# Layer 2's quotients: from two VectorE instructions to eight ScalarE ones, in a task of their own

## The chip, the cores and the metric

The kernel runs on one core of one Trainium2 chip. The metric is the device time of one execution in microseconds (us). A core has several engines, each with its own queue of instructions that it works through in order: TensorE (PE, matrix products; PEld is its weight loading), VectorE (DVE), ScalarE (ACT, which evaluates func(scale x + bias)), GpSimd (POOL) and SyncE (SP, which issues DMAs). Engines wait for one another through semaphores. PE writes its products into PSUM, from which DVE and ACT read.

## The reference

Four graph layers run one after another over x of shape (16, 1024, 64) with one 1024x1024 adjacency. Each is `x = layernorm(x + layer(x))`. Layers 0 and 2 are graph attention with an additive score:

```
h = x @ W;  s1 = h @ a1;  s2 = h @ a2
e = leaky_relu(s1[:, :, None] + s2[:, None, :], 0.2)
attention = softmax(where(adj > 0, e, NEG), axis=-1)
x = layernorm(x + elu(attention @ h))
```

Layer 1 averages softplus features with a softmax of their own over the neighbours, and layer 3 is a four-head attention with scores h h^T followed by an output attention. The change lies in layer 2.

## The kernel before

**Layers.** `fast_path` computes layers 0 to 3 in sequence; a general path behind a flag is not taken with these inputs. In the profile layer 2 lies between 461 and 688 us, and layer 3 takes the rest.

**Layer 2's work.** `gat_layer` is used for layers 0 and 2; layer 2 has `zero_mean=True`. Nodes lie on 128 partitions in C=8 chunks of 128. For one batch b there are eight *units*, one for each chunk k of source nodes: DVE makes `e = max(G, q) * aT` of 128x1024 (L965), where G and q hold the exponentials that factor exp(leaky_relu(s1+s2)) and aT is the transposed adjacency. PE then multiplies `vals` (x weighted by p) with e into a PSUM accumulator y (L977). After eight units the batch has its unnormalised result, and a list of *ends* finishes it:

- `evict`: ACT copies y from PSUM to SBUF (L996)
- `project`: PE multiplies by the weight, eight products of 128x130 into a PSUM tile `po`, columns 128 and 129 being the sums of the softmax (L1009)
- `divide`: DVE clamps the sums (L1034) and takes reciprocals rt (L1036), two DVE multiplications make the quotients v = po*rt (L1039), and ACT makes m = exp(v) (L1046)
- `residual`: two DVE operations, elu and x added (L1051, L1052)
- `norm`: DVE's bn_stats for eight chunks (L1060); for an odd b also the moments of both batches of a pair
- `root`, `shift`: for an odd b, ACT's Ln and Exp for the inverse root (L703, L704), and DVE's refinement and shift
- `store`: ACT writes the normalised x, eight activations of 128x64 (L776)

**Preparation.** For each pair of batches: `prep_x` (PE transposes, ACT copies, L904, L905), `prep_s` (PE, L911), `prep_top` (DVE maximum, then a reduction over partitions on POOL, L922), `prep_p` (DVE L928, L930, ACT exponentials p and q, L933, L935), `prep_G` in two halves (PE product pg, L945, and ACT exponential into G, L946; pg has one buffer), and `prep_v` (ACT, eight activations with a pointer scale, L952, and a copy, L954). The first e of an even batch needs both halves of G.

**Order.** The order on every engine is the order of the program, written out by hand in slots (t, k): t is the round, 0 to 16, and k the unit, 0 to 7. In slot (t, k) DVE makes unit k of batch t, PE multiplies the unit made two units before (LAG = 2), and then the tasks of the slot are issued: ends first, by batch, then preparation, then extras. An end of batch b at place (1, 4) is issued in slot (b+1, 4). Ends with places after the parameter `own` in round 16 (5 before) are handed on and issued in the first bursts of layer 3. Layer 3's first preparation is in slots (15, 0) to (15, 7), and the last rows of layer 1 in (0, 0) to (1, 7).

The places of the preparation for a pair starting at b, relative to b, are:

```
places = (-2, 0), (-2, 1), (-2, 5), (-2, 6), (-2, 7), (-1, 1), (-1, 4), (-1, 6), (-1, 2), (0, 4)
```

in the order prep_x 0 and 1, prep_s lower and upper, prep_top, prep_p, prep_G 0 and 1, prep_v of b and of b+1.

Of the kernel before, what the change touches and what calls it, by code (L numbers as in the profile page):

```python
# [12 lines left out]
AF = mybir.ActivationFunctionType  # L13
# [565 lines left out]
def fast_path(  # L579
# [24 lines left out]
    nc = tc.nc  # L604
# [8 lines left out]
    CH = C // 2  # L613
# [136 lines left out]
    def moments(st):  # L750


        n = st.shape[1]
        t = {k: small.tile([P, n], F32, tag=f"bn_{k}", name=f"bn_{k}") for k in ("mean", "d", "var", "rstd", "shift")}
        v = nc.vector
        v.tensor_tensor(t["d"], st[:, :, 1], st[:, :, 4], ALU.subtract)
        v.tensor_tensor(t["var"], st[:, :, 2], st[:, :, 5], ALU.add)
        v.tensor_tensor(t["mean"], st[:, :, 1], st[:, :, 4], ALU.add)

        v.scalar_tensor_tensor(t["d"], t["d"], 0.25, t["d"], ALU.mult, ALU.mult)  # L760
        v.tensor_scalar(t["var"], t["var"], 1.0 / D, LN_EPS, ALU.mult, ALU.add)
        v.tensor_tensor(t["var"], t["var"], t["d"], ALU.add)
        root, step = inverse_root(t["rstd"], t["var"])

        def finish():
            step()
            v.scalar_tensor_tensor(t["shift"], t["mean"], -0.5, t["rstd"], ALU.mult, ALU.mult)  # L767
            return t["rstd"], t["shift"]

        return root, finish  # L770
# [114 lines left out]
    def gat_layer(w, name, zero_mean, extra, first, own, ordered):  # L885
# [74 lines left out]
        def attention(b):  # L960
            held = {}
# [69 lines left out]
            def divide():  # L1031
                pos, tot = held["p"]
                total = sums[:, b, :]
                nc.vector.tensor_scalar(total.rearrange("p (h t c) -> p t c h", h=2, t=2), tot, 1e-30, None, ALU.max)  # L1034
                rt = small.tile([P, C], F32, tag="rt", name="rt")
                nc.vector.reciprocal(rt, total)  # L1036
                held["v"] = ep.tile([P, C, D], F32, tag="v", name="v")
                for h, po in enumerate(pos):
                    nc.vector.tensor_tensor(  # L1039
                        held["v"][:, h * CH : (h + 1) * CH, :].rearrange("p (t c) d -> p t c d", t=2), po,  # L1040
                        rt[:, h * CH : (h + 1) * CH].rearrange("p (t c) -> p t c", t=2).unsqueeze(3).to_broadcast(
                            [P, 2, 2, D]
                        ), ALU.mult,
                    )
                held["m"] = ep.tile([P, C, D], F32, tag="m", name="m", bufs=4)
                nc.scalar.activation(held["m"], held["v"], AF.Exp)  # L1046
# [25 lines left out]
            def store():  # L1072
                rows = slice(b % 2 * C, (b % 2 + 1) * C)
                scaled(xb(b), held["m"], [t[:, rows] for t in stats[b // 2]["n"]], range(C))

            return unit, product, [evict, project, divide, residual, norm, root, shift, store]

# [3 lines left out]
        def at(t, k, task):  # L1083
            slots.setdefault((t, k), []).append(task)

        work = [attention(b) for b in range(B)]
        if zero_mean:
            ends = [(1, 1), (1, 3), (1, 4), (1, 6), (1, 7), (2, 0), (2, 2)]
            ends = [*ends, (3, 6)], [*ends, (3, 2)]
        else:  # L1090

            ends = (
                [(1, 3), (1, 5), (1, 7), (2, 0), (2, 1), (2, 1), (2, 1), (4, 0)],
                [(1, 3), (1, 7), (2, 1), (2, 2), (2, 3), (2, 5), (2, 7), (3, 4)],
            )
# [28 lines left out]
        for t in range(B + 1):  # L1124
            for k in range(C):
                catch_up()
                if t < B:
                    unit, product, _ = work[t]
# [348 lines left out]
    with tc.tile_pool(name="ps_g", bufs=1, space=bass.MemoryType.PSUM, reuse_waits="tile") as ps_g, tc.tile_pool(  # L1477
        name="ps_u", bufs=2, space=bass.MemoryType.PSUM, reuse_waits="tile"
    ) as ps_u, tc.tile_pool(name="gat0", bufs=2, reuse_waits="tile") as gp:
        later = {}  # L1480

        def first(ahead):
            with tc.tile_pool(name="stage", bufs=2, reuse_waits="tile") as stage:
                tiles = load_adj(stage)
                load_x(2)
                load_x(3)
                later["w2"] = gat_weights(L2_W, L2_a, "l2", True, nc.sync)
                later["w3"] = layer3_weights(gp)
                for b in range(4, B):
                    load_x(b)  # L1490
                for c in range(C):
                    adjacency(stage, tiles[c], c)
                    for task in ahead[c : c + 1]:
                        task()
                for task in ahead[C:]:
                    task()

        extra = {(0, 6): [lambda: gat_setup(later["w2"], "l2", True)], (1, 2): [lambda: later["w3"]()]}
        ending = gat_layer(w_0, "l0", False, extra, first, 5, True)
# [14 lines left out]
    with tc.tile_pool(name="l1", bufs=2, reuse_waits="tile") as l1, tc.tile_pool(  # L1514
# [55 lines left out]
        def product_l1(g, ic):  # L1570
            po = ps_a.tile([P, 2, 2, P], F32, tag="acc", name=f"po{g}_{ic}")
            for k in range(C):
                for e in (his[g], los[g]):
                    nc.tensor.matmul(  # L1574
                        po.rearrange("p q k f -> p (q k f)"), aR[:, k, ic * P : (ic + 1) * P],
                        e[:, k].rearrange("p q k f -> p (q k f)"),
                        start=(k == 0 and e is his[g]), stop=(k == C - 1 and e is los[g]),
                    )
            return po
# [15 lines left out]
        for g in range(NG):  # L1595
            ahead = prep_l1(g + 1) if g + 1 < NG else [[] for _ in range(C)]
            st = l1.tile([P, C * GB, 6], F32, tag="st1", name=f"st{g}")
            for ic in range(C):
                po = product_l1(g, ic)
# [6 lines left out]
            root, finish = moments(st)  # L1606
# [30 lines left out]
    for b in range(B):  # L1637
# [6 lines left out]
        ends = outs[b][1][1]  # L1644
# [37 lines left out]
    with tc.tile_pool(name="ps_g", bufs=1, space=bass.MemoryType.PSUM, reuse_waits="tile") as ps_g, tc.tile_pool(  # L1682
        name="ps_p", bufs=1, space=bass.MemoryType.PSUM, reuse_waits="tile"
    ) as ps_p, tc.tile_pool(
        name="gat2", bufs=2, reuse_waits="tile"
    ) as gp:
        places = [(15, j) for j in (0, 1, 2, 3, 4, 5, 6, 7)]
        extra = {p: [task] for p, task in zip(places, ahead)}
        for p, task in zip(((0, 0), (0, 1), (0, 3), (0, 7), (1, 3), (1, 7)), last):
            extra.setdefault(p, []).append(task)  # L1690

        def first(ahead):
            for task in ahead:
                task()

        ending = gat_layer(later["w2"], "l2", True, extra, first, 5, True)
    for j, task in enumerate(ending):
        at(0, j, task)

# [81 lines left out]
def kernel(tc, *args):  # L1781


    nc = tc.nc
    with tc.tile_pool(name="flag", bufs=1) as fp:
        redo = fp.tile([1, 1], I32, tag="redo", name="redo")
        fast_path(tc, redo, *args)
        again = nc.values_load(redo[0:1, 0:1], min_val=0, max_val=1)
        with tc.If(again == 1):
            general_path(tc, *args)  # L1790
# [32 lines left out]
```

## Time and profile before

| | |
|---|---|
| median of three runs | 2103.89 us (2102.4 to 2103.98) |
| profiled execution, its own time | 2103.7 us |
| its span, first to last instruction | 2101.4 us |
| busy over the span: PE, DVE, ACT | 94%, 88%, 59% |
| layer 2's e (L965 covers layers 0 and 2) | 256 times, 1277 ns each |
| quotients, L1039 (layers 0 and 2: L1039 is 64 instructions) | 24.2 us |

A row of a group names the line, engine and operation, output <- inputs with shapes, the count, then busy us and the mean ns of one, then the time its engine sat idle just before it and what ended that. The mean of one instruction is longer than the distance between two in a row, because an engine starts the next before the last is through. A row of the timeline has start and length in us, then the same names; neighbouring instructions of a kind are merged (x5). An idle time and its releaser stand in brackets.

### The profile page before, as it was taken

How to read it: one execution, taken by the hardware profiler on the slowest of the kernel's cores; microseconds unless marked ns; L12 is line 12 of the kernel's file. 1: busy time of each engine (PE TensorE's matmuls, PEld its weight loads, DVE VectorE, ACT ScalarE, POOL GpSimd, SP SyncE). 2: the span in 40 equal slices, each digit the busy share in tenths (PEclk: the TensorE clock that was granted, in tenths of full speed). 3: DMA queues.
4: the chain of work that ended last, by engine and by line, in shares of the span. 5: the costliest groups of instructions: out<-in, count | busy, mean ns of one | idle time of the engine just before them, and what ended most of it. 6: DMA issues, size and time to landing. Idle time of an engine off the chain costs nothing.

```text
span 2101.4 us, 26433 instructions
## 1 busy us (share of the span) xinstructions
PE 1969.2 (94%) x10065; PEld 858.0 (41%) x10065; DVE 1845.0 (88%) x3160; ACT 1237.7 (59%) x2029; POOL 69.7 (3%) x77
## 2 busy tenths in 40 slices
PE   6999979989888999999999999999999999999983
PEld 3444347863332343343434334333434343433431
DVE  5888989989999778798898898989989889888997
ACT  4355556645555766666666656656665665665541
POOL 0000000000000000000000000000000000000001
PEclk7999989999999999999999999999999999999997
DMA  7000000000000100000000000000000000000000
GB/s 167 1 1 1 1 1 1 1 1 1 0 1 11 51 21 1 1 1 6 1 5 6 1 6 1 6 6 1 6 1 6 6 1 6 6 1 6 1 5 17
DMA packets 23656, 18.91 MB, mean 9 GB/s; under 512 B 19361, under 2 KB 19426, under 8 KB 23522
## 3 DMA queue, kind: packets, MB, share of 16 engines
q1 hardware_dynamic: 23218, 17.11, 3.0%
q8 instruction: 81, 1.33, 0.3%
q14 instruction: 53, 0.43, 0.1%
q10 hardware_dynamic: 304, 0.03, 0.0%
HBM read 12.95 MB, written 4.19 MB: 8 GB/s over the span
## 4 chain that ended last, share of the span: by engine, by line
PE 45%; DVE 41%; ACT 10%; issue 3%; DMA 0%; POOL 0%; SPq 0%; POOLq 0%; DVEq 0%; ACTq 0%
DVE e L1290 12%; PE y L1297 11%; PE s L1282 8%; DVE e L965 7%; ACT e L1286 6%; PE y_l L977 6%; DVE junk L1392 4%; DVE e L1403 4%; PE u_l L989 3%; PE po L1574 3%; PE po L1312 2%; PE y L1412 2%; ACT e L1387 2%; DVE v L1322 1%; PE s L1382 1%
## 5 line engine op out<-in xcount | busy, mean ns | idle before, releaser
L1286 ACT ACTIVATE e<-s,shift 128x1024 f32<-128x1024 f32 x512 | 542.8, 1119 | 335.0 <-PE s L1282 334.2
L1290 DVE TENSOR_TENSOR e<-e,aT 128x1024 f32<-128x1024 f32 x512 | 600.4, 1217 | 1.7 <-ACT e L1286 1.6
L1282 PE MATMUL s<-hT 64*128 64x512 f32 x2048 | 495.1, 603 | 1.2 <-ACT e L1286 0.9
L1297 PE MATMUL y<-e,vals 128*64 128x512 f32 x2048 | 488.7, 599 | 5.8 <-ACT yT L1303 4.3
L965 DVE SCALAR_TENSOR_TENSOR e<-G_l,q,aT 128x1024 f32<-128x1024 f32 x256 | 315.3, 1277 | 7.2 <-ACT G_l L946 7.2
L1282 PEld LDWEIGHTS s<-hT 64*128 64x128 f32 x2048 | 185.7, 186 | 278.0 <-issue 138.9
L977 PE MATMUL y_l<-e,vals_l 128*64 128x512 f32 x1024 | 261.2, 634 | 25.3 <-DVE e L965 24.4
L1297 PEld LDWEIGHTS y<-e,vals 128*64 128x64 f32 x2048 | 134.7, 136 | 272.4 <-issue 190.7
L1392 DVE SCALAR_TENSOR_TENSOR junk<-e,aN 128x1024 bf16<-128x1024 f32 x128 | 155.8, 1217 | 0.0
L1403 DVE TENSOR_TENSOR e<-e,aT 128x1024 f32<-128x1024 f32 x120 | 147.0, 1225 | 6.4
L1387 ACT ACTIVATE e<-s,shift 128x1024 f32<-128x1024 f32 x128 | 142.1, 1116 | 1.2 <-PE s L1382 1.1
L1382 PE MATMUL s<-h2T 64*128 64x512 f32 x512 | 131.6, 595 | 0.0
L977 PEld LDWEIGHTS y_l<-e,vals_l 128*64 128x64 f32 x1024 | 64.8, 141 | 162.5 <-issue 73.1
L1412 PE MATMUL y<-e,h2v 128*64 128x512 f32 x480 | 123.4, 592 | 2.7 <-DVE e L1403 2.7
L1574 PE MATMUL po<-hi,aR 128*128 128x512 f32 x256 | 101.9, 398 | 2.7 <-ACT hi L1559 1.1
L1574 PE MATMUL po<-lo,aR 128*128 128x512 f32 x256 | 99.8, 390 | 0.0
L776 ACT ACTIVATE x<-m,bn_shift,bn_rstd 128x64 f32<-128x64 f32 x256 | 88.3, 430 | 0.5 <-DVE bn_shift L767 0.5
L1225 POOL PARTITION_ALL_REDUCE gtop<-top x48 | 42.5, 885 | 1367.0 <-DVE top L1223 1298.8
L1312 PE MATMUL po<-wb,yT 128*128 128x130 f32 x512 | 74.2, 288 | 10.1 <-ACT e L1286 9.4
L1312 PEld LDWEIGHTS po<-wb,yT 128*128 128x128 f32 x512 | 61.9, 190 | 47.4 <-ACT e L1286 45.8
L1382 PEld LDWEIGHTS s<-h2T 64*128 64x128 f32 x512 | 49.7, 188 | 61.2 <-issue 28.8
L1316 DVE COPY sums<-po 128x8 f32<-128x8 f32 x64 | 10.9, 170 | 71.8 <-PE po L1312 71.8
(217 smaller groups left out, 2059.1 us busy)
## 6 DMA issues: line engine op xcount, KB each, us to landing
adj<-in_adj_dram SPq DMA_DIRECT2D x16, 512.0 KB, 4.2
x<-in_x_dram SPq DMA_DIRECT2D x16, 256.0 KB, 5.2
out_dram<-res SPq DMA_DIRECT2D x16, 256.0 KB, 2.0
wl<-in_L_gnn_Wh_dram SPq DMA_DIRECT2D x2, 64.0 KB, 3.6
wo<-in_L_gnn_Wo_dram SPq DMA_DIRECT2D x1, 64.0 KB, 3.1
l_wd<-in_L_gnn_W_dram ACTq DMA_DIRECT2D x2, 16.0 KB, 3.9
l_wd<-in_L_gnn_W_dram SPq DMA_DIRECT2D x2, 16.0 KB, 2.0
bo<-in_L_gnn_bo_dram SPq DMA_DIRECT2D x1, 32.0 KB, 3.1
```

The lines of the kernel that those rows point to most:

```text
L965: nc.vector.scalar_tensor_tensor(e, G[b - b % 2][:, b % 2, :], pq[b - b % 2][1][:, k, b % 2 : b % 2 + 1], aT[:, k, :], ALU.max, ALU.mult,)
L977: nc.tensor.matmul(held["y"][h * D : (h + 1) * D, :], vals[b][:, k, :], e[:, h * HALF : (h + 1) * HALF], start=(k == 0), stop=(k == C - 1),)
L1282: nc.tensor.matmul(s[:, i, :], hT[rows, k * P : (k + 1) * P], hT[rows, cols], start=True, stop=True)
L1286: nc.scalar.activation(e, s, AF.Exp, bias=shifts[b, n])
L1290: nc.vector.tensor_tensor(e, e, bc_mid(aT[:, k, h * HALF : (h + 1) * HALF], 2), ALU.mult)
L1297: nc.tensor.matmul(held[h][i * D : (i + 1) * D, :], vals[b][:, k, :], e[:, i, :], start=(k == 0), stop=(k == C - 1),)
L1312: nc.tensor.matmul(o[:, j // 2, j % 2, :], held["y"][:, j * P : (j + 1) * P], wb[:, n, :], start=True, stop=True,)
L1382: nc.tensor.matmul(s[:, i, :], hT[rows, (i + k // CH) % 2, k % CH * P : (k % CH + 1) * P], hT[rows, 0, :], start=True, stop=True,)
L1387: nc.scalar.activation(e, s, AF.Exp, bias=shifts[b])
L1392: nc.vector.scalar_tensor_tensor(junk.rearrange("p c q -> p (c q)").bitcast(BF16), e.rearrange("p i q -> p (i q)"), 1.0, aN[:, k, :], ALU. ...
L1403: nc.vector.tensor_tensor(m, e, aT[:, k, :].rearrange("p (i q) -> p i q", i=2), ALU.mult)
L1574: nc.tensor.matmul(po.rearrange("p q k f -> p (q k f)"), aR[:, k, ic * P : (ic + 1) * P], e[:, k].rearrange("p q k f -> p (q k f)"), start ...
```

## The change

In layer 2 `divide` keeps the clamp and the reciprocal. The quotients become a task `quotients` of their own: eight ACT activations (Copy with the scale taken from a column of rt) from PSUM into v, then m = exp(v) as before. In layer 0, `divide` calls `quotients` at once and nothing else differs. The places of layer 2's ends are new: evict (1,1), project (1,3) and divide (1,4) stay; quotients (1,5); residual from (1,6) to (2,0); norm from (1,7) to (2,1); for odd b root from (2,0) to (2,3), shift from (2,2) to (2,5), store from (3,2) to (3,4); for even b root and shift do nothing, and the store goes from (3,6) to (4,0). `own` goes from 5 to 6, so that the last batch's quotients still belong to layer 2. The same six tasks as before are handed on to layer 3.

```diff
                 nc.vector.reciprocal(rt, total)
                 held["v"] = ep.tile([P, C, D], F32, tag="v", name="v")
+                held["r"] = rt
+                if not zero_mean:
+                    quotients()
+
+            def quotients():
+                pos, rt = held["p"][0], held["r"]
                 for h, po in enumerate(pos):
+                    if zero_mean:
+
+                        for j in range(CH):
+                            c = h * CH + j
+                            nc.scalar.activation(
+                                held["v"][:, c, :], po[:, j // 2, j % 2, :], AF.Copy, scale=rt[:, c : c + 1]
+                            )
+                        continue
                     nc.vector.tensor_tensor(
                         held["v"][:, h * CH : (h + 1) * CH, :].rearrange("p (t c) d -> p t c d", t=2), po,
...
-            return unit, product, [evict, project, divide, residual, norm, root, shift, store]
+            ends = [evict, project, divide, residual, norm, root, shift, store]
+            if zero_mean:
+                ends.insert(3, quotients)
+            return unit, product, ends
...
         if zero_mean:
-            ends = [(1, 1), (1, 3), (1, 4), (1, 6), (1, 7), (2, 0), (2, 2)]
-            ends = [*ends, (3, 6)], [*ends, (3, 2)]
+            ends = [(1, 1), (1, 3), (1, 4), (1, 5), (2, 0), (2, 1)]
+            ends = [*ends, (2, 1), (2, 1), (4, 0)], [*ends, (2, 3), (2, 5), (3, 4)]
...
-        ending = gat_layer(later["w2"], "l2", True, extra, first, 5, True)
+        ending = gat_layer(later["w2"], "l2", True, extra, first, 6, True)
```

## The prediction

> **What bounds the kernel now.** I read the page first, then busy time by stretch, to find layer 2 (461 to 688 us), then its waits and groups, and last the timeline of one pair of batches. By stretch (columns: length; busy PE, PEld, DVE, ACT, POOL; granted PE clock; DMA):
>
> ```profile
> 484.94:654.86 169.92, 147.70 (x672) 55.51 (x668) 167.09 (x359) 92.62 (x272) 7.41 (x6) 0.94 0.00 1
> 654.86:687.73 32.87, 26.73 (x128) 9.70 (x128) 29.54 (x73) 19.80 (x55) 1.59 (x2) 0.95 0.06 17
> ```
>
> The first row is six pairs of batches (t=2 to 13), 28.32 us each: VectorE (DVE) is busy 98%, ScalarE (ACT) 55%. The second is t=14 to the first exponential of layer 3. What DVE waited for in the first row, and groups of that row:
>
> ```profile
> DVE l_sums L1034 <- PE po L1009: 0.3, 1, 0.3
> ...
> L965 DVE SCALAR_TENSOR_TENSOR e<-G_l,q,aT 128x1024 f32<-128x1024 f32 x96 | 118.6, 1277 | 0.0
> L952 ACT ACTIVATE vals_l<-x,p 128x63 f32<-128x63 f32 x96 | 24.0, 332 | 0.0
> L1039 DVE TENSOR_TENSOR v<-po,rt 128x256 f32<-128x256 f32 x24 | 9.1, 419 | 0.4
> L1046 ACT ACTIVATE m<-v 128x512 f32<-128x512 f32 x12 | 7.6, 631 | 36.4 <-DVE v L1039 36.4
> ```
>
> DVE waits once, 0.3 us in 170. So layer 2 is a DVE queue without gaps, and a DVE instruction taken out shortens it until something else arrives late. The candidate stands in the timeline, second half of a pair (t odd):
>
> ```profile
> 506.06 0.17 DVE L1034 TENSOR_SCALAR l_sums<-po 128x8 f32<-128x8 f32 x1
> 506.16 1.13 PE L945 MATMUL pg<-xT_l,l_w 64*128 64x512 f32 x4
> 506.26 0.20 DVE L1036 RECIPROCAL rt<-l_sums 128x8 f32<-128x8 f32 x1
> 506.50 0.76 DVE L1039 TENSOR_TENSOR v<-po,rt 128x256 f32<-128x256 f32 x2
> 507.17 2.47 DVE L965 SCALAR_TENSOR_TENSOR e<-G_l,q,aT 128x1024 f32<-128x1024 f32 x2
> 507.29 0.63 ACT L1046 ACTIVATE m<-v 128x512 f32<-128x512 f32 x1 [2.96 <-DVE v L1039]
> 507.83 1.10 ACT L946 ACTIVATE G_l<-pg,up 128x1024 f32<-128x1024 f32 x1
> 508.82 2.75 ACT L776 ACTIVATE x<-m,bn_shift,bn_rstd 128x64 f32<-128x64 f32 x8
> 511.48 1.09 ACT L946 ACTIVATE G_l<-pg,up 128x1024 f32<-128x1024 f32 x1
> 513.11 6.05 DVE L965 SCALAR_TENSOR_TENSOR e<-G_l,q,aT 128x1024 f32<-128x1024 f32 x5
> ```
>
> The next pair's first e (513.11) reads all of G, whose second half ends at 512.57: 0.54 us to spare. Last, the end of the layer, where ACT carries the path, and the PE clock in two stretches:
>
> ```profile
> 684.08 0.57 ACT L996 COPY yT_l<-y_l 128x512 f32<-128x512 f32 x1
> 684.55 2.76 ACT L776 ACTIVATE x<-m,bn_shift,bn_rstd 128x64 f32<-128x64 f32 x8
> ...
> 687.21 0.61 ACT L1046 ACTIVATE m<-v 128x512 f32<-128x512 f32 x1
> 687.73 5.10 ACT L1286 ACTIVATE e<-s,shift 128x1024 f32<-128x1024 f32 x5
> ```
> ```profile
> 498.94:500.94 2.00, 0.27 (x2) 0.30 (x4) 1.97 (x5) 0.82 (x3) 1.24 (x1) 0.85 0.00 0
> 500.94:502.94 2.00, 2.00 (x6) 0.48 (x5) 2.00 (x4) 1.12 (x5) 0.00 (x0) 0.50 0.00 0
> ```
>
> **The change, part by part.** Below, t is the round of the loop and times are starts, in us.
>
> *Removed from DVE.* Two quotients a batch. From l_sums to the next e it is 506.06 to 507.17, 1.11 us; without the quotients the e follows the reciprocal's start by about 0.10 (independent small operations start 0.10 apart), so 0.30. Saved: 0.81 a batch, 1.62 a pair.
>
> *Added on ACT.* Eight activations with one pointer scale. Nearest row: L952, eight of 128x63 with one pointer, 2.00 us, 0.2375 apart. Upper end: L776, two pointers, eight from 508.82 to 511.48, 0.333 apart. Lower end: ACT copies 128x512 from PSUM in 576 to 599 ns against 631 for L1046 from SBUF, so up to 0.045 less, 0.19. The operation is L952's, so I take 0.2375, 2.00 for eight. The exponential starts 0.03 later (L703 and L704, dependent, start 0.24 apart with 0.216 each) and lets the next in after 0.54. ACT's load becomes 15.4+2x1.9=19.2 of 26.6 us a pair, 72%: no bound by volume.
>
> The Trainium skill, "ScalarE: Activation LUTs", Rules for kernel authors, says to give a multiplication to VectorE, not ScalarE. Per element the rows agree (0.84 us on DVE, 2.00 on ACT), and by that rule alone the sum would be 16x(2.00-0.81)=19 us slower, an estimate that takes all of it as exposed.
>
> *Moved.* Residual, bn_stats, root, shift and store come one to two slots later. Their instructions are the same; no DMA moves, and POOL's reduction stays. What matters is what they no longer cover. At t odd DVE had, between the divide and the next pair's first e, three e's, the residual (1.33: 509.56 to 510.89) and bn_stats (1.02). Now residual and bn_stats come before e1 and e2, and the shift (0.71) comes after e5. The new t odd, e's 1.195 apart (chain: 5.97 for five): e0 at 0, residual 1.20, e1 2.53, bn_stats and moments 3.72 (2.02), down/up 5.74 (0.13), e2 5.87, e3 7.07, e4 8.26, divide 9.46, e5 9.76, shift 10.95, e6 11.66, e7 12.86, and the next e0 at **14.05**. The new t even is 12.51 (e's 9.56, residual 1.33, bn_stats 1.02, divide 0.30, top 0.30). The pair: 26.56 against 28.17, the undisturbed period (484.94 to 513.11).
>
> *The new wait.* When is G ready? PE takes product(e2) 0.05 after e2 ends (5.87+1.28), 7.20; pg follows 1.01 later (505.15 to 506.16), 8.21, lasts 1.13; first half of G on ACT at 9.39. ACT is free then: p, q and eight vals from 5.92 to 8.34, root to 8.85. Then, in ACT's order: quotients at 9.39+0.99=10.38 (the reciprocal was done at 9.86), exponential 12.41, second half of G 12.95, done 14.05, seen by DVE 14.09 (0.04 as at 461.11 to 461.15). Wanted at 14.05: a wait of **0.04** a pair. Slack has gone to nothing, and every further us is paid six times. What queues behind the quotients on ACT is that half of G; who waits is e0, and behind it all DVE.
>
> At t even nothing waits: two stores, copies and vals hold ACT until 8.9, the quotients follow the reciprocal (8.7), m is ready near 11.6, and the residual wants it at 13.7. PE, at t even, does 12.0 of work in 12.51 and its backlog drains in t odd.
>
> *Start.* At t=1 no residual yet stands before the divide (it ran at 477.90), so e0 of t=2 is wanted at 477.90+0.30+3x1.195=481.79. ACT: rows of x at 476.77 end 479.42, G's first half, quotients 480.41, exponential 482.44, second half 482.98 to 484.08, seen 484.12. The wait is 2.33; e0 comes at 484.12 instead of 484.94: -0.82, while residual and bn_stats of batch 0 (2.35) are still owed.
>
> *Six pairs.* 6x(28.17-26.56)=-9.66, and 6x0.04=+0.24 waits.
>
> *End.* Before, 32.87 from t=14's first e to layer 3's first exponential. Now t=14 is 12.21; in t=15 e7 is at about 12.9 and the second maximum at 14.1. ACT then: its shift 14.83 (POOL between), the store of batch 12 (now behind it; it ran at 680.10 in ACT's idle time) 15.03, yT 17.68, store of 13 at 18.15 to 20.80, quotients of 15 (reciprocal ready at 19.9), exponential 22.83, layer 3's first at 23.37. Sum 35.58: **+2.71**. It holds the owed 2.35 on DVE, which ACT's queue covers.
>
> Sum: -0.82-9.66+0.24+2.71=**-7.5 us**. Layer 3 starts that much earlier and runs on unchanged. The profiled execution took 2103.7 (span 2101.4, and 2.3 around it), 0.2 below the median of 2103.89: 2103.7-7.5=**2096.2**.
>
> With x the extra time of a batch's eight quotients over 2.00, the total is -7.5+8x: six pairs, start and end all pay it. Pitch 0.333 gives x=0.76, 2102.3; pitch 0.19 gives start and end 0.37 each and the waits of 0.24 back, 2095.2.
>
> **Rivals.** 0.2% is 4.2 us, about what a measurement here can tell from no change.
>
> *A, within 0.2%: G late by half a us to 1.4 in each pair.* Through x above 0.41, or through PE at half clock. The two clock rows show 0.50 after PE had sat 2.53 us before one product; that gap (bn_stats and moments with nothing else) is gone. The new gaps, 1.28 before product(e1) and 1.25 before product(e2), are shorter than 1.64 (before 650.73), after which it stayed 1.00, but the clock did fall after 1.70 (before 669.76). If it falls at product(e2), that and pg (1.7 and 1.84 in slow rows) put G 1.4 late: -7.5+6x1.4, 2104.6. The Trainium skill, "TensorE: Matmul & The Clock Gate", Part 1, throttles only after an idle window of about 3.4 us; by that it would not fall here, yet the trace has it falling after 2.53.
>
> *B, slower: the quotients do not overlap.* They write one tile out of shared banks and might run one after another as L703 and L704 do. At L952's 0.332+0.03 each, x=0.9, 2103.4, still A; at L776's 0.430+0.03, x=1.65, 2109.4. It decides from a pitch of about 0.42, x=1.46. Against it: L952's eight also write one tile, and overlap.
>
> *C, ACT is the path throughout.* The quotients' 2.00 is paid where 0.81 was saved, 19 us over sixteen batches: 2122.7. Against it: at t even m has two us to spare, and ACT's 55%. This is the ScalarE rule's outcome.
>
> **How the numbers follow.** My forecast 0.64, all of it faster; A 0.18, within (x from 0.41 to 1.46, or G late by as much); B 0.14, slower (x above 1.46); C 0.04, slower. Faster 0.64, same 0.18, slower 0.18. The forecast's own range is 2093 to 2099.5: x from -0.3 to 0.4, and an end between +1 and +3.5. For eight in ten the range reaches through A to 2106; below 2092.5 I leave 0.03.
>
> **What would show it.** Quotients 0.24 apart on ACT; a pair of about 26.6 us; e0 of each even batch waiting for G under 0.3 us, 2.3 at t=2; no 2.5 us PE gap; layer 3's first exponential near 680.2. Wrong if e0 waits over 1 us for G in every pair, if the clock is 0.50 at product(e2), or if DVE waits for a residual's m.

## The result

The changed kernel takes 2096.86 us (median of six, 2093.37 to 2097.86) against 2103.14 for the kernel before: ratio 0.9964, 95% interval 0.9952 to 0.9977. Two repeats beside the experiments gave 0.9961 (0.9948 to 0.9975) and 0.9972 (0.9962 to 0.9982). The profiled execution has a span of 2095.2 us, 6.2 less than before.

By stretch, columns as in the prediction; the first row is again t=2 to 13, the second t=14 to layer 3's first exponential (L1303 now), the third the 12.3 us behind it:

```profile
483.13:642.73 159.60, 140.67 (x672) 53.26 (x669) 157.46 (x334) 111.11 (x365) 7.42 (x6) 0.99 0.00 1
642.73:678.20 35.47, 27.19 (x132) 9.10 (x132) 29.49 (x77) 27.66 (x86) 1.88 (x2) 0.95 0.06 16
678.20:690.50 12.30, 11.38 (x44) 4.08 (x40) 9.95 (x10) 11.20 (x14) 0.00 (x0) 0.85 0.00 0
```

Six pairs take 159.60 us instead of 169.92, the end 35.47 instead of 32.87. VectorE is still busy 98.7% of the first row, ScalarE now 70%. The groups of that row and all that VectorE waited for in layer 2 (461 to 690 us):

```profile
L952 ACT ACTIVATE vals_l<-x,p 128x63 f32<-128x63 f32 x96 | 24.0, 337 | 0.0
L1049 ACT ACTIVATE v<-po,rt 128x64 f32<-128x64 f32 x96 | 21.0, 333 | 4.2 <-DVE rt L1036 4.2
```
```profile
DVE e L1307 <- ACT e L1303: 5.1, 4, 3.9
DVE l_sums L1034 <- PE po L1009: 3.0, 1, 3.0
DVE e L965 <- ACT G_l L946: 2.3, 1, 2.3
DVE l_s L918 <- PE ps L911: 0.5, 1, 0.5
```

The wait for G (L965 on L946) occurs once, at t=2. In the pairs after it G is just in time. The wait for ps (L918) belongs to t=1; it was not there before the change. The timeline of a t odd:

```profile
505.00 1.11 ACT L946 ACTIVATE G_l<-pg,up 128x1024 f32<-128x1024 f32 x1 [0.59 <-PE pg L945]
505.07 0.16 DVE L1034 TENSOR_SCALAR l_sums<-po 128x8 f32<-128x8 f32 x1
505.26 0.21 DVE L1036 RECIPROCAL rt<-l_sums 128x8 f32<-128x8 f32 x1
505.38 1.24 DVE L965 SCALAR_TENSOR_TENSOR e<-G_l,q,aT 128x1024 f32<-128x1024 f32 x1
506.01 1.74 ACT L1049 ACTIVATE v<-po,rt 128x64 f32<-128x64 f32 x8
...
507.25 3.67 DVE L965 SCALAR_TENSOR_TENSOR e<-G_l,q,aT 128x1024 f32<-128x1024 f32 x3
507.78 0.63 ACT L1060 ACTIVATE m<-v 128x512 f32<-128x512 f32 x1
508.32 1.10 ACT L946 ACTIVATE G_l<-pg,up 128x1024 f32<-128x1024 f32 x1
```

The e after the reciprocal starts at 505.38, 0.31 after l_sums. Of the three e's from 507.25, 1.195 apart, the third begins the next pair at 509.64; G's second half ends at 509.42. The slack is 0.22 us. (The rows are those of ScalarE and VectorE alone.)

At the end of the layer ScalarE's two stores (L776) stand ahead of the last quotients, and the products of layer 3 (L1299) wait for PSUM until ScalarE has read it:

```profile
670.16 2.74 ACT L776 ACTIVATE x<-m,bn_shift,bn_rstd 128x64 f32<-128x64 f32 x8
672.81 0.56 ACT L996 COPY yT_l<-y_l 128x512 f32<-128x512 f32 x1
673.28 2.76 ACT L776 ACTIVATE x<-m,bn_shift,bn_rstd 128x64 f32<-128x64 f32 x8
673.43 1.16 PE L1009 MATMUL po<-l_wo,yT_l 128*128 128x130 f32 x8 [3.26 <-ACT yT_l L996]
...
675.94 1.70 ACT L1049 ACTIVATE v<-po,rt 128x64 f32<-128x64 f32 x8
677.67 0.63 ACT L1060 ACTIVATE m<-v 128x512 f32<-128x512 f32 x1
677.69 5.73 PE L1299 MATMUL s<-hT 64*128 64x512 f32 x16 [1.52 <-ACT v L1049]
```

The sixteen products took 5.73 us, against 3.77 us for the same sixteen before: the granted clock was 0.50 from 677.69 to 681.00, where before it was 1.00. Layer 3 makes its exponentials in bursts of five. From its first exponential to the first of its second burst it was 8.42 us, against 6.98 before.

### The profile page after: what moved, and what is told of

Its sections match the earlier page's. It is cut to its first block, busy times and chain, and to the rows that moved or that the text cites. A ratio compares the mean times of both kernels' runs of the same rounds, so it can differ in the third digit from the quotient of the medians.

```text
span 2095.2 us, 26536 instructions
## 1 busy us (share of the span) xinstructions
PE 1970.0 (94%) x10065; PEld 859.3 (41%) x10065; DVE 1832.4 (87%) x3128; ACT 1265.0 (60%) x2157; POOL 70.0 (3%) x77
## 3 DMA queue, kind: packets, MB, share of 16 engines
q8 instruction: 81, 1.33, 0.3%
## 4 chain that ended last, share of the span: by engine, by line
PE 46%; DVE 40%; ACT 10%; issue 3%; DMA 0%; POOL 0%; SPq 0%; POOLq 0%; DVEq 0%; ACTq 0%
DVE e L1307 12%; PE y L1314 11%; PE s L1299 9%; DVE e L965 7%; ACT e L1303 6%; PE y_l L977 6%; DVE junk L1409 4%; DVE e L1420 4%; PE u_l L989 3%; PE po L1591 3%; PE po L1329 2%; PE y L1429 2%; ACT e L1404 2%; DVE v L1339 1%; PE s L1399 1%
## 5 line engine op out<-in xcount | busy, mean ns | idle before, releaser
L1303 ACT ACTIVATE e<-s,shift 128x1024 f32<-128x1024 f32 x512 | 543.1, 1119 | 336.1 <-PE s L1299 335.3
L1299 PE MATMUL s<-hT 64*128 64x512 f32 x2048 | 497.6, 605 | 2.4 <-ACT v L1049 1.5
L965 DVE SCALAR_TENSOR_TENSOR e<-G_l,q,aT 128x1024 f32<-128x1024 f32 x256 | 314.7, 1274 | 10.3 <-ACT G_l L946 10.3
L1299 PEld LDWEIGHTS s<-hT 64*128 64x128 f32 x2048 | 186.3, 186 | 281.2 <-issue 140.2
L977 PE MATMUL y_l<-e,vals_l 128*64 128x512 f32 x1024 | 255.8, 621 | 25.0 <-DVE e L965 23.2
L776 ACT ACTIVATE x<-m,bn_shift,bn_rstd 128x64 f32<-128x64 f32 x256 | 88.3, 430 | 0.5 <-DVE bn_shift L767 0.5
```

Source lines behind the costliest of these rows:

```text
L965: nc.vector.scalar_tensor_tensor(e, G[b - b % 2][:, b % 2, :], pq[b - b % 2][1][:, k, b % 2 : b % 2 + 1], aT[:, k, :], ALU.max, ALU.mult,)
L977: nc.tensor.matmul(held["y"][h * D : (h + 1) * D, :], vals[b][:, k, :], e[:, h * HALF : (h + 1) * HALF], start=(k == 0), stop=(k == C - 1),)
L1299: nc.tensor.matmul(s[:, i, :], hT[rows, k * P : (k + 1) * P], hT[rows, cols], start=True, stop=True)
L1303: nc.scalar.activation(e, s, AF.Exp, bias=shifts[b, n])
```

## The experiments

Executions scatter by a few us, so beside each time I give a length from the trace: from layer 2's first e on VectorE to layer 3's first exponential. It is 226.58 us for the kernel before, and 218.66, 217.76 and 218.00 in three profiles of the changed one.

**The changed kernel again.** No edit.

> The changed kernel again, beside the three that follow, so that they can be compared with it on one chip. Both theories: 6 to 7.5 us below the kernel before (about 2096.5 where before has 2103). Layer 2 gains about 8.5 us up to the first exponential of layer 3, and the first five exponentials of layer 3 lose about 1.4 of it while TensorE's clock is low.

2093.74 us against 2102.02. Layer 2 gained 8.8 us in this profile (217.76), as expected. The loss of 1.4 at the start of layer 3, which was expected again, was not there: the second burst came 6.98 after the first, as before. It is not a fixed price of the change.

> The changed kernel again, for comparison with the three that follow on the same chip: 6 to 7.5 us below the kernel before.

2095.17 against 2102.70; the second burst came 7.61 after the first.

**The new places without ScalarE's quotients.**

```diff
-                    if zero_mean:
+                    if False:
```

> Places of the change, but the quotients stay two VectorE instructions (now after e5). Theory (the gain is 0.81 us of VectorE time a batch in a queue without gaps): a pair takes 26.56+1.62 = 28.2 us again, the first e of a pair does not wait for G, the end of the layer is 1 to 1.5 us longer than before; in all within 2 us of the kernel before, 2102 to 2105. Rival (the gain comes from the new places, which take away TensorE's 2.5 us gaps and lift its clock in layer 2 from 0.94 to 0.99): at least half of the gain stays, 2100 or less.

2101.74 against 2102.02, ratio 0.9999 (0.9990 to 1.0008); 225.55 us. The gain is gone, and the rival with it, for PE's clock is 0.99 in the six pairs here too:

```profile
480.34:647.89 167.55, 144.00 (x676) 52.88 (x672) 165.42 (x359) 91.18 (x271) 7.41 (x6) 0.99 0.00 1
```

The VectorE rows show what a quotient costs in the new place:

```profile
572.45 1.23 DVE L965 SCALAR_TENSOR_TENSOR e<-G_l,q,aT 128x1024 f32<-128x1024 f32 x1
573.60 0.74 DVE L1053 TENSOR_TENSOR v<-po,rt 128x256 f32<-128x256 f32 x2
574.27 1.27 DVE L965 SCALAR_TENSOR_TENSOR e<-G_l,q,aT 128x1024 f32<-128x1024 f32 x1
```

Both quotients take 573.60 to 574.27, 0.67. A pair is 27.83 us (G's second half at 534.26, 562.08, 589.91), which is 26.50+2x0.67. Before it was 28.17: of the 1.67 saved in a pair, 1.33 comes from handing the quotients to ScalarE and 0.34 from the new places. Most of the 0.34 is that VectorE starts an e 0.12 after the reciprocal's start, where the quotient came 0.24 after it, twice a pair. One part of the expectation missed: the end of the layer, from t=14 to layer 3, is 3.4 longer than before (36.23 against 32.87), not 1 to 1.5. So the longer end belongs to the new places, with or without ScalarE's quotients.

**ScalarE's quotients at the old places.**

```diff
-            ends = [(1, 1), (1, 3), (1, 4), (1, 5), (2, 0), (2, 1)]
-            ends = [*ends, (2, 1), (2, 1), (4, 0)], [*ends, (2, 3), (2, 5), (3, 4)]
+            ends = [(1, 1), (1, 3), (1, 4), (1, 4), (1, 6), (1, 7), (2, 0), (2, 2)]
+            ends = [*ends, (3, 6)], [*ends, (3, 2)]
...
-        ending = gat_layer(later["w2"], "l2", True, extra, first, 6, True)
+        ending = gat_layer(later["w2"], "l2", True, extra, first, 5, True)
```

> Quotients on ScalarE directly after the reciprocal in slot (1,4), all other ends at their old places. Theory: 0.81 us a batch saved on VectorE, but the second half of G comes behind the quotients and a store: quotients 506.6 to 508.3 in the times of the kernel before, exponential, first half of G 508.9, store 509.9, second half 512.5 to 513.6, wanted at 513.11-0.81 = 512.3, so each of six pairs waits about 1.3 us, 7.8 in all; the end pays 1.7 for the last quotients. In all 2 to 4 us below the kernel before, 2099 to 2101. Rival (the new places do nothing): the whole gain is there, 2096 to 2097.

2108.29 against 2102.02, ratio 1.0028 (1.0016 to 1.0041): slower, which neither theory had said. In one pair:

```profile
564.91 0.69 DVE L1065 SCALAR_TENSOR_TENSOR v<-v,x 128x512 f32<-128x512 f32 x1 [0.20 <-ACT m L1060]
...
568.44 1.10 ACT L946 ACTIVATE G_l<-pg,up 128x1024 f32<-128x1024 f32 x1
...
569.57 6.07 DVE L965 SCALAR_TENSOR_TENSOR e<-G_l,q,aT 128x1024 f32<-128x1024 f32 x5 [1.02 <-ACT G_l L946]
```

The wait for G is 1.02 a pair where I expected 1.3, and each residual waits 0.2 for m. With two residuals that is 1.4 of the 1.62 saved in a pair, and a pair takes 28.18, as before. The last 0.2 fits the overlap that is lost at a wait: before, the e at 513.11 starts 0.08 before the end of the bn_stats ahead of it (513.19), so each of the three waits delays VectorE by about 0.08 more than it lasts. I had priced both ends of the layer too low. The first e of t=2 comes 24.71 us after the layer's first e, against 23.79: the quotients stand on ScalarE behind layer 1's rows, so the first residual waits 1.18 for m, and the e then 0.40 for G, whose second product PE cannot make before G's first half has left pg. From t=14 to layer 3 it is 36.39 against 32.87. With the six pairs (170.70) that sums to 231.80 against 226.58. So the quotients on ScalarE pay only because of the new places, and the places alone gain nothing.

**Twice the quotients.** Two kernels repeat each quotient activation. The first repeats each at once, the second runs all eight and then all eight again.

```diff
-                        for j in range(CH):
+                        for j in [j for j in range(CH) for _ in range(2)]:
```
```diff
-                for h, po in enumerate(pos):
+                for h, po in [*enumerate(pos)] * (2 if zero_mean else 1):
```

> The changed kernel with each of the eight quotient activations issued twice (the second writes the same values again), 1.6 to 1.75 us more on ScalarE a batch. Theory (ScalarE's order before G is the path at three places, with only 0.2 us to spare in a pair): the first e of a pair waits about 1.45 us six times, and start and end pay 1.65 each: 12 us slower than the changed kernel, 2107 to 2110, above the kernel before. Rival (ScalarE is busy 70% of layer 2 and hides it): within 2 us of the changed kernel.

2129.09 us (2123.35 to 2135.14), 35 over the changed kernel where 12 were expected (28 over it in the trace). ScalarE was not hidden, but the size was wrong. The timeline of one pair shows the row of sixteen and the wait behind it:

```profile
568.81 4.51 ACT L1049 ACTIVATE v<-po,rt 128x64 f32<-128x64 f32 x16
...
575.02 1.28 DVE L965 SCALAR_TENSOR_TENSOR e<-G_l,q,aT 128x1024 f32<-128x1024 f32 x1 [2.49 <-ACT G_l L946]
```

Sixteen took 4.51, not 3.4: 2.77 more than eight. Layer 2 up to layer 3 is 245.70.

> As e3_twice, but all eight quotients first and then all eight again, so that no activation writes the place that the one just before it wrote. Theory (in e3_twice sixteen took 4.51 us instead of the 3.4 counted on because each second one waited for the first to end, 0.36 against 0.20 apart): sixteen take 3.3 to 3.5 us, the extra is 1.6 to 1.75; with 0.2 us to spare each of six pairs waits 1.4, start and end pay 1.65 each, 11 to 13 us over the changed kernel, 2105 to 2108. Rival (a second reading of the same PSUM costs more whatever the order): sixteen take 4.5 us again and the time is 2120 or more.

2108.33 us (2105.65 to 2116.68) against 2102.69, ratio 1.0036 (1.0022 to 1.0049). In turn, sixteen take 3.38, so a second reading is not dearer in itself:

```profile
535.62 3.38 ACT L1049 ACTIVATE v<-po,rt 128x64 f32<-128x64 f32 x16
...
539.57 1.10 ACT L946 ACTIVATE G_l<-pg,up 128x1024 f32<-128x1024 f32 x1
```
```profile
540.70 1.28 DVE L965 SCALAR_TENSOR_TENSOR e<-G_l,q,aT 128x1024 f32<-128x1024 f32 x1 [1.37 <-ACT G_l L946]
```

With 1.64 us more on ScalarE the pair waits 1.37 for G, so it swallowed about 0.25, and grows from 26.50 to 27.96. With the 2.77 more of the kernel before this one the wait was 2.49: about 0.3 swallowed. Layer 2 up to layer 3 is 231.12, 13 more than the changed kernel's 218.1. That is the chain of the prediction, with its slack, measured at two lengths: by both, ScalarE, though busy only 70%, sets the time once its quotients are 0.2 to 0.3 us longer.

**The start.** The two last groups of rows of layer 1 moved behind the first G.

```diff
-        for p, task in zip(((0, 0), (0, 1), (0, 3), (0, 7), (1, 3), (1, 7)), last):
+        for p, task in zip(((0, 0), (0, 1), (0, 3), (0, 7), (2, 0), (2, 4)), last):
```

> The changed kernel with layer 1's last two groups of rows at (2,0) and (2,4), where ScalarE has no stores yet, instead of (1,3) and (1,7). Theory (the 2.3 us wait for G at the first e of t=2 is ScalarE's 2.65 us of rows standing before G): the wait goes, and 2 to 2.3 us less than the changed kernel, about 2094.5. Rival (another wait takes its place): less than 0.7 us.

2095.06 against 2095.17 for the changed kernel beside it: no difference to be seen. In the trace 217.05 against 218.00, 0.95 less where 2 to 2.3 were expected:

```profile
476.60 1.12 ACT L946 ACTIVATE G_l<-pg,up 128x1024 f32<-128x1024 f32 x1 [1.74 <-PE pg L945]
477.61 1.74 ACT L1049 ACTIVATE v<-po,rt 128x64 f32<-128x64 f32 x8
...
479.92 1.10 ACT L946 ACTIVATE G_l<-pg,up 128x1024 f32<-128x1024 f32 x1
481.05 1.28 DVE L965 SCALAR_TENSOR_TENSOR e<-G_l,q,aT 128x1024 f32<-128x1024 f32 x1 [1.23 <-ACT G_l L946]
```

With the rows away ScalarE idles 1.74 us for PE's product pg, which stands in PE's order behind the projection and a product. The wait for G is 1.23, against 1.99 in the changed kernel beside it (2.32 in the first profile).

**The end.** The stores of batches 12 and 13 are handed on to layer 3.

```diff
             for task, (t, k) in zip(work[b][2], ends[b % 2]):
+                if zero_mean and B - 4 <= b < B - 2 and task is work[b][2][-1]:
+                    t, k = B + 4 - b, b % 2
                 at(b + t, k, task)
...
-        return [task for t in range(B, B + 3) for k in range(C) for task in slots.get((t, k), []) if (t, k) >= (B, own)]
+        return [task for t in range(B, B + 5) for k in range(C) for task in slots.get((t, k), []) if (t, k) >= (B, own)]
```

> The changed kernel with the stores of batches 12 and 13 handed on to layer 3's bursts 6 and 7, behind the six tasks already there. Theory (at the end of layer 2 two stores of 2.65 us stand on ScalarE before the last quotients): the first exponential of layer 3 comes 3.5 to 4 us sooner after the first e of t=14, TensorE's gap there shrinks and its clock holds, so another 0.5 to 1.4: 4 to 5.3 us less than the changed kernel, about 2092. Rival (the stores are only put off and are paid in layer 3, or another chain ends as late): less than 2 us.

2090.68, 4.5 less than the changed kernel beside it, ratio to before 0.9943 (0.9930 to 0.9956). Layer 2 up to layer 3 is 214.46, 3.5 less, and the second burst of layer 3 follows after 6.97. No store stands in front of yT or of the last quotients any more, and ScalarE even waits for the latter:

```profile
669.71 0.59 ACT L996 COPY yT_l<-y_l 128x512 f32<-128x512 f32 x1
672.05 1.75 ACT L1049 ACTIVATE v<-po,rt 128x64 f32<-128x64 f32 x8 [1.75 <-DVE ok L1777]
```

PE's idle time before the last projection shrinks from 3.26 to 0.69, and the sixteen products of layer 3 take 3.80.

In a repeat the trace gave nearly the same, 214.51; the times spread more (2089.15 to 2099.5):

> The kernel with the last two stores handed on, again, to stand beside the two that follow: 11 to 12.5 us below the kernel before.

2093.81 against 2102.69, 0.9967 (0.9954 to 0.9979): 8.9 below the kernel before, where 11 to 12.5 were expected.

> Both edits together. Theory: they lie at different ends of the layer and add up, 6 to 7.6 us less than the changed kernel, about 2090, 13 to 14 below the kernel before. Rival: 3 us or less.

2090.71, ratio 0.9942 (0.9929 to 0.9955). That is 4.5 under the changed kernel beside it, not the 6 to 7.6 expected. In the trace it is 213.72, 0.7 less than the end's edit alone; in the times nothing, as the start's edit is worth little.

**Both ends on VectorE.** As the end's edit, and the quotients of the first and the last batch stay on VectorE.

```diff
-                    if zero_mean:
+                    if zero_mean and 0 < b < B - 1:
```

> As e5_end, and the quotients of batches 0 and 15 stay on VectorE, all others on ScalarE. Theory (at start and end ScalarE is the path, and VectorE waits 2.3 and 3.1 us): the wait for G at t=2 goes, 2.3 less 0.7 of VectorE work; the last quotients take 0.7 instead of 1.75: 2.5 to 2.8 us less than e5_end, 2087.5 to 2088.5. Rival (other work ends as late at both places): less than 1 us.

2091.68 (2086.07 to 2095.49) against 2093.81 for the kernel with the end's edit beside it, ratio to before 0.9950 (0.9934 to 0.9966). In the trace 212.53, 2.0 less than 214.51 where 2.5 to 2.8 were expected, about half of it at each end; the wait at t=2 is down to 0.41. The times are too spread to tell 2 us. By the trace it is the shortest layer 2 of all, 14 us under the kernel before.

## Why the prediction was right

The forecast was 2096.2 with a gain of 7.5; measured were 6.3, 8.3 and 7.5 in the three comparisons. The mechanism held, but that the total comes so close is partly luck. Against the one profile of the kernel before, in us, for the profiled execution and the two repeats:

| stretch | counted | measured | repeats |
|---|---|---|---|
| before layer 2's first e | 0 | -1.61 | -0.52, -2.01 |
| from there to the first e of t=2 | -0.82 | -0.20 | -1.11, -1.11 |
| six pairs | -9.42 | -10.32 | -10.31, -10.26 |
| from t=14 to layer 3's first exponential | +2.71 | +2.60 | +2.60, +2.79 |
| from there to the end | 0 | +3.33 | +1.74, +1.49 |
| span | -7.5 | -6.2 | -7.6, -9.1 |

Layer 2 itself gained 7.9 to 8.8, a little more than the 7.5 counted, and something in layer 3 took part of it back. The first row holds nothing that the change touches: the layer's first e comes between 457.89 and 461.15 in all thirteen profiles, and the kernel before, with one profile, happens to be the latest. Mostly for that reason layer 3's first exponential came at 678.20, not near 680.2. Step by step:

- *Saved on VectorE.* 0.81 a batch: the pair is 26.50 in the undisturbed middle (G's second half at 508.32, 534.83, 561.32), 26.56 was counted. The six pairs gained 0.9 more than counted because the sum started from the undisturbed pair of 28.17, while two of the six before took 28.53 and 28.71. The experiment with the new places alone shows that the gain is this and not PE's clock, which rose from 0.94 to 0.99 with the new places alone as well.
- *The quotients.* I took 2.00 us for eight; they took 1.74, near the lower bound of 0.19 apart (1.74 for eight is 0.20 apart, the last one lasting 0.33).
- *The wait of G.* 0.04 counted, none seen. G's first half began 0.07 before l_sums, as computed; the shorter quotients left 0.22 to spare.
- *The start.* A wait of 2.33 counted, 2.32 measured in the first profile and 1.98 and 1.99 in the repeats. In the first profile VectorE also waited 0.49 for ps at t=1, which the prediction had not counted; so the stretch gained only 0.20 there. The cause of the wait for G was told only in part: behind the rows stands PE's pg, as the experiment on the start shows.
- *The end.* +2.71 counted, +2.60 measured, and the two stores are its cause: handing them on gave back 3.5 in the trace. The new places alone, without ScalarE's quotients, made the end 3.4 longer.
- *Layer 3 "runs on unchanged".* This step was wrong in the profiled execution. PE idles 3.26 us before the last projection, and after it the granted clock is 0.50 for a while in all three profiles; how much of this falls into the sixteen products of layer 3 differs, and it cost 1.44, 0 and 0.63. The rest of the difference lies further on: from the reduction at 700.54 (708.62 before) to the end it is 1.9 us longer than before in the profiled execution, and 1.7 and 0.8 in the repeats. No run shows that this is a price of the change: over the same length, with the same layer 3, the kernel with the new places alone was 0.1 shorter than the kernel before and the one with the old places 2.0 longer. What makes these differences is open.
- *The rivals.* A's late G did not come, and neither did a low clock at product(e2): in the six pairs the granted clock is below 1.00 only between 626.77 and 630.76 (0.57), where no product(e2) lies and no wait followed. B's quotients overlap: eight in 1.74 us at 0.333 each. (B was to decide from a pitch of about 0.42; 2.00 and x=1.46 for eight come to 0.43 to 0.45, which changes nothing here.) C is excluded by the middle of the layer. But the kernel with the quotients at the old places shows that a path through ScalarE was near: there it did cost what was saved.
- *The formula -7.5+8x.* With 1.64 more for the quotients the trace grew by 13.0; the formula gives 13.1 and, less six times the slack, about 11.6. Against the first profile of the changed kernel, which waited as long before its first e (5.91), it grew by 12.5: 9.2 in the six pairs, 1.7 at the start and 1.6 at the end. So it held to about one us, and the closer agreement of 13.1 with 13.0 is luck, as the formula leaves the slack out.

The Trainium skill, "ScalarE: Activation LUTs", Rules for kernel authors, puts a multiplication on VectorE, not ScalarE. By that rule alone the prediction estimated a slower kernel; the runs disagree, at 0.9961 to 0.9972 of the time before.

## What to carry to other kernels

When one engine's queue has no gaps, an operation can be worth moving off it even to an engine that needs more than twice as long (here 1.74 us in place of 0.67 to 0.81), but only if what the second engine produces next still comes in time: lay out both queues over one period and read off the slack at each crossing. Here the move and the new places were worth nothing or less alone, and 0.3 to 0.4% together. The start and the end of the pipelined layer had another critical engine than its middle (ScalarE, not VectorE), and the placing that suited the middle was paid for there; here the last stores were the ones worth handing on.

## What the runs showed of the hardware that I had not expected

Activations of 128x64 out of PSUM with one pointer scale follow each other at 0.20 us, against 0.2375 for 128x63 out of SBUF. An activation that repeats the one just before it, with the same source and the same place to write, comes later: two on one place averaged 0.56 (4.51/8), against 0.42 (3.38/8) when the same sixteen ran in turn. Whether the shared source or the shared place makes it is not shown.

PE's granted clock also fell without a long idle time. In layer 2 each pair of batches has two groups of eight narrow products (L911, 128x4). In six of eleven profiles (those with twice the quotients left aside) the clock fell to about 0.50 once in the six pairs, each time within 0.2 us of the end of the second group: at 551.4 before, at 627.0 in the first profile of the change. In the latter PE had not stood idle for more than 0.56 us at a stretch since 610. The other sixty of these 66 places passed without a fall; what decides is not shown. It cost nothing there: the pair took 27.10, as in a repeat without the fall.
